# Moving the scaling of s, a piece of statistics, silu stores and a load of gates, and merging two copies of u, in a bidirectional scan layer

## The chip, the cores and the metric

The kernel runs on one core of one Trainium2 chip. The metric is the device time of a whole launch in microseconds (us). The profile is one execution recorded by the hardware profiler. Engines are named as in its views: PE is TensorE's matmul, PEld its weight load, ACT ScalarE, DVE VectorE, POOL GpSimd, SP (or SPq) SyncE, which here issues nearly all transfers.

## The reference

The input x has 4 images of 128 channels and 96 x 96 pixels. It is group-normalised (32 groups), read as four sequences of 9216 positions (rows forward, rows backward, columns forward, columns backward), and each goes through the same layer:

```python
t = grouped1x1(x, in_proj_w, in_proj_b, 4)        # 128 -> 512 channels
u, gate = t[:, :256], t[:, 256:]
u = silu(u)
u = depthwise_conv(u, dw_w, K=5)
s  = ssm_in_w @ u                                  # 256 -> 32, as the next three
a  = clip(0.999 + 0.0009 * sigmoid(ssm_delta_w @ u + b), 0.0001, 0.9999)
bb = tanh(ssm_b_w @ u + b)
cc = tanh(ssm_c_w @ u + b)
prefix = cumsum(log(a))
h = exp(prefix) * cumsum(bb * s * exp(-prefix))    # h[n] = a[n] * h[n-1] + bb[n] * s[n]
u = u + ssm_out_w @ (cc * h + ssm_d * s)
u = grouped1x1(u * sigmoid(gate), mix_w, mix_b, 4)
y = out_proj_w @ u + out_proj_b
```

The four results are put back in pixel order, joined to 512 channels, multiplied by `fuse_w` (128 x 512), and added to x.

## The kernel before, in words

**Tiling.** All data is fp32. The work of an image is two phases, vertical ("V", columns) and then horizontal ("H", rows); so there are 8 phases, numbered 0 to 7. Each phase runs two streams side by side: s = 0 reads the sequence forward, s = 1 the same sequence backward. A phase has 6 steps (`NS`), and a step has four pairs (`R`). A pair is a tile of 384 positions (every fourth position of 1536) of both streams. So there are 24 pairs in a phase and 192 in all, numbered t = 0 to 191; k is t mod 4.

**Second halves are not computed anew.** The backward stream meets in the second half of a phase what the forward stream met in the first, and the other way round. So in_proj with its silu (`compute_front`, L476) and the gates (`gate`, L487, `sigmoids`, L509) run only for steps 0 to 2 of a phase ("fresh"). Gates of the first ten pairs of a phase are stored to DRAM (L518) and loaded back for their mirrored pairs (`load_kept`, L526); the last two pairs' gates stay in two buffers, `gates[0]` and `gates[1]`, which the loads use too. The silu of steps 0 and 1 is stored (`keep_silu`, L452, 770 KB for a quarter of a step) and loaded back (`load_silu`, L458). The silu tile `sil` has two buffers, so step 2 is written where step 0 was.

**One pair.** `pair(t)` works on pair t at its front end and on pair t - 6 (`LAG`) at its back end. "old" means that the back end's pair is in the second half of its phase, "with_front" that in_proj for pair t + 4 runs here, and "ahead" that the pair is old or has no in_proj. By position in a phase, pairs 20 to 23 and 0 to 5 are old with in_proj, 6 and 7 have in_proj and gates, 8 to 17 have gates and no in_proj, and 18 and 19 are old without in_proj. The parts of a pair, with their names and lines, are:

- `front`: in_proj of pair t + 4 into banks 7, 6, 2, 3, its silu on ACT (L476), loads of the next step's x_in (L252), and stores of silu.
- `taps` (L611, DVE, and L609, ACT): the convolution's second half of the channels, five taps. The first tap is written to PSUM by ACT a pair ahead (`first_tap`).
- `conv` and `conv_less`: the first half of the channels as matmuls with banded matrices ("band", then "less"), L133 being the helper that records every matmul of 32 columns. L594 copies the results of both streams to SBUF as u.
- `proj` (L133, "main"): the four small projections into banks 4 and 5, read by ACT as tm (L639), a copy of s (L640) and a tanh (L641). POOL makes a of it (L644) and bb * s (L647), and `scale_s` (L664, ACT) then multiplies s by ssm_d in place.
- `scan` (L681, DVE), two calls a step, and `outputs` (L687 to L689, POOL), five pairs later.
- `out_of` (L493): ssm_out_w into banks 0 to 3, onto u that ACT has copied there (`under`, L501).
- `gating` (L563, DVE), reading gates and banks 0 to 3. Banks 0 and 1 are also those of the first tap, so ACT's first tap waits for it.
- `accumulate` (L133, "w_fin"): mix, out_proj and fuse_w in one product, copied by ACT as ys (L712, L714) and added to acc by POOL (L728).

**What sets the order.** The order of instructions on each engine is written out by hand: the pairs run under a manual schedule, so each engine and SyncE's queue carry out instructions in the order in which the program names them. Only semaphores between engines are added.

**Banks.** With in_proj, `conv` uses banks 4 and 5 (`PROJ`); without it banks 7 and 6 (`FRONT[:2]`), stream 0 in bank 7 and stream 1 in bank 6. The gates of such a pair go to banks 4, 5, 7, 6 (`GATE[False]`), so the third and fourth gate matmul wait until u has been copied out of 7 and 6.

**Statistics.** The next image's normalisation is prepared on the side: in V phases chunks of x are loaded (L393) and reduced (L397, DVE) in pairs with k > 1, and `stats_finish` is a generator whose pieces are called in the H phase, one in each pair with k > 1 (`stats_piece`); some of the pieces have matmuls (L186, L198, L234).

The lines that decide where the changed parts stand are these:

```python
if ahead:
    accumulate(waiting.pop(0), w[1])()
    free[0] = w[0]
    stats_piece()

    other = nc.vector.tensor_copy if k > 1 and not old else nc.scalar.copy
    conv_less(i, banks, (nc.scalar.copy, other))
...
    first_tap(i + 2)
    scale_s(i - 2)
```

Of the kernel before, what the change touches and what calls it, by code (L numbers as in the profile page):

```python
# [55 lines left out]
R = 4  # L56
LN = 16
NS = HH // LN
N = LN * WW // R
# [7 lines left out]
def conv_preact_kernel(  # L67
# [60 lines left out]
    def bank(i):  # L128
        return psum[:, i, :]

    def mm(o, col, lhsT, rhs, start, stop):
        r = slice(32 * col, 32 * col + 32)
        nc.tensor.matmul(o[r, : rhs.shape[-1]], lhsT, rhs, start=start, stop=stop,  # L133
                         skip_group_check=True)
# [183 lines left out]
    def less_of(p):  # L318
        return 1 if p < 2 else 0
# [93 lines left out]
    def front(i, banks):  # L413
        for _ in front_parts(i, banks):
            pass

    def front_parts(i, banks):

        step, g = divmod(i, R)
        if step * UB >= NU:  # L420
            return
        st = step % NS
        if st == NS // 2:
            sils[step] = sils[step - 1]
            load_silu(step + 1, (g,))
        elif st == NS - 1 and g < 2:
            load_silu(step, (2 * g, 2 * g + 1))
        elif g == 0 and fresh(step):
            sils[step] = wk.tile([P, 2, 2, 4, N + 1], F32, tag="sil", name=f"sil_{step}")
        if fresh(step):  # L430
            yield from compute_front(step, g, banks)
        sil = sils[step]

        if st == 0:
            engine = nc.gpsimd if step else nc.vector
            for s in range(2):
                engine.memset(sil[64 * s : 64 * s + 64, s, 0, g, 0:1], 0.0)
            if g < 2:
                engine.memset(sil[:, :, 1, g, 0:1], 0.0)

        for s in range(2):
            load_front(step + 1, s, slice(64 * s + 32, 64 * s + 64), slice(g, g + 1))
        if g == R - 1:
            for s in range(2):
                load_front(step + 1, s, slice(64 * s, 64 * s + 32), slice(0, R))
        if step:
            keep_silu(step, g)

    def keep_silu(step, g):
        st = step % NS  # L450
        if st < NS // 2 - 1:
            nc.sync.dma_start(kept_sil[step // NS % 2][st][g], sils[step][:, :, :, g, :])  # L452

    def load_silu(step, gs):
        if 0 in gs:
# [111 lines left out]
    def columns(step, sil, k):  # L567

        if fresh(step):
            return sil[..., k : k + N]  # L570
        return sil[..., 1 - k : 1 - k + N][..., ::-1]

    def blocks(step):
        return [sils[step][:, s if fresh(step) else 1 - s, 0] for s in range(2)]

    def conv(i, banks):

        step, p = units[i]["step"], units[i]["p"]
        sil, k = blocks(step), less_of(p)
        for s in range(2):  # L580
            for g in range(4):
                mm(bank(banks[s]), g, band[:, s, p, g, :], columns(step, sil[s][:, g, :], 1 - k),
                   True, False)

    def conv_less(i, banks, copies=(nc.scalar.copy, nc.scalar.copy)):
        step, p = units[i]["step"], units[i]["p"]
        sil, k = blocks(step), less_of(p)
        for g in range(4):
            for s in range(2):
                r = less_rows(s, p)  # L590
                mm(bank(banks[s]), g, less[r, p, g, :], columns(step, sil[s][r, g, :], k),
                   False, True)
        for s, copy in enumerate(copies):
            copy(us[i][:, s, 0, :], bank(banks[s])[:, :N])  # L594

    def new_u(i):
        us[i] = wk.tile([P, 2, 2, N], F32, tag="u", bufs=LAG + 2, name=f"u_{units[i]['id']}")
# [64 lines left out]
    def scale_s(i):  # L662
        s = tbs[i][0:64, :]
        nc.scalar.activation(s, s, AF.Copy, scale=d_sb[0:64, 0:1])  # L664
# [68 lines left out]
        return add  # L733


    later = []

    waiting = []

# [7 lines left out]
    def pair(t):  # L747
# [9 lines left out]
        banks, w = plan(with_front or not back)  # L757
        if back:
            front(t + R, FRONT)
        if seed and not with_front:  # L760
            under(bi, 1)
        send()
# [19 lines left out]
        def stats_piece():  # L782
            if later and k > 1:
                next(later[0], None)
# [11 lines left out]
        if ahead:  # L796
            accumulate(waiting.pop(0), w[1])()
            free[0] = w[0]
            stats_piece()

            other = nc.vector.tensor_copy if k > 1 and not old else nc.scalar.copy
            conv_less(i, banks, (nc.scalar.copy, other))
        if old:
            for s in range(2):
                for j in range(2):
                    out_of(bi, s, j)
                load_gate(bi + s + UB)
        elif back:
            gates_and_out(bi, with_front)
# [168 lines left out]
```

## Time and profile before

| | |
|---|---|
| time, median of 3 runs | 1869.76 us (1868.79 to 1873.79) |
| span of the profiled execution | 1866.4 us, mean granted TensorE clock 0.990 |
| busy: PE, DVE, ACT, POOL | 98%, 84%, 83%, 84% |
| bytes read and written in DRAM | 185 MB and 132 MB, 170 GB/s over the span |
| silu stores and loads (L452, L458) | 128 of 770 KB, 6.2 us to landing |
| stores of gates (L518) | 80 of 768 KB, 3.9 us |
| loads of kept gates (L526) | 76 of 768 KB, 5.0 us |
| copies of u (L594) | 352 on ACT, 482 ns; 32 on DVE, 550 ns |
| copy of 128x768 on ACT (L501) | 352, 802 ns |
| scaling of s (L664) | 192, 601 ns |

A row of the profile's groups names line, engine, operation, the tile written and those read, shapes and count; then the busy time, the mean of one, and the idle time of its engine just ahead of it with what ended it. A row of the timeline is a start, a duration, the engine, the line and the tiles, "xN" for several in a row, and in brackets the idle time before. A matmul of fp32 shows as two records. Durations of matmuls include the time in which the next one already runs, so what a group costs is read from start to start.

### The profile page before, as it was taken

The numbers are of one execution on the slowest core, as the hardware profiler recorded it, in microseconds if no ns is written. First come the engines' busy times: TensorE is split into PE (matmuls) and PEld (weight loads), VectorE is DVE, ScalarE is ACT, GpSimd is POOL, SyncE is SP. The second block draws the span as 40 slices with busy tenths as digits, with TensorE's granted clock in tenths as the row PEclk, the third lists the DMA queues.
The fourth block names the chain that finished last, engine by engine and source line by source line (L and its number), as shares of the span: only waits on it lengthen the run. The fifth ranks groups of instructions, "written<-read, shape, count | busy, mean of one in ns | idle before, by whom it ended". The sixth has DMA issues, their size and how long they took to land.

```text
span 1866.4 us, 57669 instructions
## 1 busy us (share of the span) xinstructions
PE 1827.3 (98%) x24024; PEld 691.4 (37%) x24024; DVE 1561.9 (84%) x1573; ACT 1542.6 (83%) x2841; POOL 1567.0 (84%) x1615
## 2 busy tenths in 40 slices
PE   6899999999999999999999999999999999999998
PEld 3234333443334433344333433334333443334432
DVE  4698878888888988888889898888887888878886
ACT  4688888888888888888888888888888888888875
POOL 6388988888879899888887989888888889997886
PEclk7999999999999999999999999999999999999999
DMA  5564463433875557243596556433467634535424
GB/s 194 162 197 145 146 207 118 168 141 126 274 244 202 169 155 215 86 158 131 186 301 217 167 162 207 152 130 126 139 224 234 231 113 156 191 118 175 145 102 171
DMA packets 147828, 321.21 MB, mean 172 GB/s; under 512 B 14192, under 2 KB 115696, under 8 KB 147568
## 3 DMA queue, kind: packets, MB, share of 16 engines
q1 hardware_dynamic: 147136, 316.56, 51.5%
q8 instruction: 190, 3.11, 0.7%
q10 hardware_dynamic: 432, 0.96, 0.1%
q14 instruction: 70, 0.57, 0.1%
HBM read 185.21 MB, written 132.25 MB: 170 GB/s over the span
## 4 chain that ended last, share of the span: by engine, by line
PE 87%; ACT 4%; POOL 3%; DVE 2%; DMA 1%; issue 1%; SPq 0%; POOLq 0%; DVEq 0%; ACTq 0%
PE psum L133 73%; PE psum L487 7%; PE psum L493 7%; ACT sil L476 1%; DMA xs<-in_xr 1%; ACT psum L609 1%; DVE u L563 1%; DVE psum L611 1%; POOL acc L728 1%; POOL t L644 1%; ACT u L594 0%; POOL t L647 0%; DMA x_in<-in_xs 0%; POOL t L687 0%; POOL t L688 0%
## 5 line engine op out<-in xcount | busy, mean ns | idle before, releaser
L611 DVE SCALAR_TENSOR_TENSOR psum<-sil,small,psum 128x768 f32<-128x768 f32 x576 | 589.0, 1023 | 39.1 <-ACT psum L609 13.5
L133 PE MATMUL psum<-u,w_fin 128*32 128x384 f32 x6144 | 535.6, 488 | 0.0
L133 PE MATMUL psum<-u,main 128*32 128x384 f32 x6144 | 534.9, 489 | 0.3 <-DVE u L611 0.3
L563 DVE SCALAR_TENSOR_TENSOR u<-gate,psum 128x768 f32<-128x768 f32 x376 | 349.9, 952 | 165.9 <-ACT u L594 91.6
L728 POOL TENSOR_TENSOR acc<-ys,acc 128x384 f32<-128x384 f32 x376 | 412.7, 1118 | 21.6 <-ACT ys L714 4.3
L687 POOL TENSOR_TENSOR t<-t,t 64x384 f32<-64x384 f32 x192 | 263.8, 1374 | 78.0 <-DVE t L681 58.0
L133 PEld LDWEIGHTS psum<-u,w_fin 128*32 128x32 f32 x6144 | 195.9, 110 | 303.3 <-issue 223.6
L501 ACT COPY psum<-u 128x768 f32<-128x768 f32 x352 | 277.6, 802 | 34.9 <-DVE u L611 28.8
L133 PE MATMUL psum<-sil,band 128*32 128x384 f32 x3072 | 291.9, 494 | 10.8 <-ACT tm L639 8.2
L133 PEld LDWEIGHTS psum<-u,main 128*32 128x32 f32 x6144 | 181.8, 109 | 324.9 <-issue 203.0
L644 POOL TENSOR_SCALAR t<-tm 64x384 f32<-64x384 f32 x191 | 177.9, 931 | 133.0 <-ACT tm L639 103.2
L688 POOL TENSOR_TENSOR t<-t,t 64x384 f32<-64x384 f32 x192 | 276.3, 1439 | 15.1
L609 ACT ACTIVATE psum<-sil,small 128x768 f32<-128x768 f32 x192 | 174.1, 907 | 104.6 <-DVE u L563 98.6
L493 PE MATMUL psum<-t,main 32*128 32x384 f32 x1536 | 240.2, 520 | 3.3 <-POOL t L688 1.5
L647 POOL TENSOR_TENSOR t<-t,tm 64x384 f32<-64x384 f32 x192 | 208.9, 1088 | 15.3
L509 ACT ACTIVATE gate<-psum,bnorm 128x384 f32<-128x384 f32 x384 | 194.8, 583 | 13.9 <-PE psum L487 7.7
L476 ACT ACTIVATE sil<-psum,bnorm 128x385 f32<-128x385 f32 x384 | 192.0, 585 | 11.7 <-DMA xs<-in_xr 5.4
L611 DVE SCALAR_TENSOR_TENSOR u<-sil,small,psum 128x768 f32<-128x768 f32 x192 | 194.9, 1015 | 7.8
L487 PE MATMUL psum<-x_in,wn 32*128 32x384 f32 x768 | 193.8, 521 | 0.5 <-ACT u L594 0.3
L594 ACT COPY u<-psum 128x384 f32<-128x384 f32 x352 | 153.1, 482 | 30.1 <-PE psum L133 21.8
L714 ACT COPY ys<-psum 128x384 f32<-128x384 f32 x287 | 132.5, 475 | 49.5 <-PE psum L133 41.5
L133 PE MATMUL psum<-sil,less 64*32 64x384 f32 x3072 | 168.8, 497 | 0.0
(87 smaller groups left out, 1642.0 us busy)
## 6 DMA issues: line engine op xcount, KB each, us to landing
sil<-sil SPq DMA_DIRECT2D x128, 770.0 KB, 6.2
kept<-gate SPq DMA_DIRECT2D x80, 768.0 KB, 3.9
gate<-kept SPq DMA_DIRECT2D x76, 768.0 KB, 5.0
x_in<-in_xs SPq DMA_DIRECT2D x192, 96.2 KB, 2.5
out<-acc SPq DMA_DIRECT2D x48, 384.0 KB, 6.1
acc<-in_xr SPq DMA_DIRECT2D x38, 384.0 KB, 6.3
xs<-in_xr SPq DMA_DIRECT2D x72, 192.0 KB, 5.1
x_in<-in_xs SPq DMA_DIRECT2D x184, 48.1 KB, 4.7
```

The source lines that it names most:

```text
L133: nc.tensor.matmul(o[r, : rhs.shape[-1]], lhsT, rhs, start=start, stop=stop, skip_group_check=True)
L476: nc.scalar.activation(sil[:, s, j, g, :], bank(banks[2 * s + j])[:, : N + 1], AF.Silu, bias=bn[:, 1:2] if j else bn[:, 4 + g : 5 + g],)
L487: nc.tensor.matmul(bank(to)[:, :N], stats[un["b"]][0][r, s, :], x_in[s][r, q, off : off + N], start=True, stop=True)
L493: nc.tensor.matmul(bank(SSM + 2 * s + j)[:, :N], w_so[r, bass.ts(j, P)], z[r, :], start=bi not in seeded, stop=True, skip_group_check=True)
L501: nc.scalar.copy(psum[:, SSM + 2 * s : SSM + 2 * s + 2, :N], us[bi][:, s])
L563: nc.vector.scalar_tensor_tensor(v, g, 1.0, pz, ALU.add, ALU.mult)
L611: nc.vector.scalar_tensor_tensor(us[i][:, :, 1, :] if k == K - 1 else part, src, w_tap[:, k : k + 1], part, ALU.mult, ALU.add,)
L644: nc.gpsimd.tensor_scalar(*op)
L647: nc.gpsimd.tensor_mul(ta[0:64, p, :], tb[0:64, :], tm[0:64, :])
L687: nc.gpsimd.tensor_mul(ta[0:64, p, :], tb[64:P, :], ta[64:P, p, :])
L688: nc.gpsimd.tensor_add(tb[0:64, :], ta[0:64, p, :], tb[0:64, :])
L728: adder.tensor_add(part, y, part)
```

## The change

The change has six edits. They leave every matmul and every byte moved as they are.

- **Stores of silu** go through a list, `to_keep`. Step 0's four stores are issued at the end of pairs 0, 1 (two) and 2, in place of one at the end of each of pairs 0 to 3. Step 1's wait until step 2's in_proj (pairs 4 to 7), one each. In later phases a store is issued at once, as before. This is to spread the transfers of the first pairs.
- **Banks of conv**: stream s is put in the lower bank plus s, so without in_proj stream 0 is in bank 6 and stream 1 in 7.
- **One copy of u**: without in_proj both banks are copied by one ACT instruction, 128 x 2 x 384, in place of two (the second on DVE in pairs with k > 1 that aren't old). With in_proj there are two copies on ACT as before.
- **Statistics' piece**: in old pairs it is called after `conv_less` and no longer ahead of it.
- **Load of kept gates**: from pairs with k = 2 it is put off to the next pair, behind that pair's in_proj and its loads of x_in (`soon`).
- **Scaling of s**: in old pairs it stands ahead of `out_of`, before the first tap; in all others behind `proj`. Before, pairs with a back end had it between the first tap and `proj`.

```diff
         if g == R - 1:
             for s in range(2):
                 load_front(step + 1, s, slice(64 * s, 64 * s + 32), slice(0, R))
-        if step:
-            keep_silu(step, g)
-
-    def keep_silu(step, g):
-        st = step % NS
         if st < NS // 2 - 1:
-            nc.sync.dma_start(kept_sil[step // NS % 2][st][g], sils[step][:, :, :, g, :])
+            to_keep.append((step, g))
+        if step > 1:
+            keep_silu(1)
+
+    to_keep = []
+
+    def keep_silu(n):
+        for step, g in to_keep[:n]:
+            nc.sync.dma_start(kept_sil[step // NS % 2][step % NS][g], sils[step][:, :, :, g, :])
+        del to_keep[:n]
...
     def conv(i, banks):
 
         step, p = units[i]["step"], units[i]["p"]
-        sil, k = blocks(step), less_of(p)
+        sil, k, b0 = blocks(step), less_of(p), min(banks)
         for s in range(2):
             for g in range(4):
-                mm(bank(banks[s]), g, band[:, s, p, g, :], columns(step, sil[s][:, g, :], 1 - k),
+                mm(bank(b0 + s), g, band[:, s, p, g, :], columns(step, sil[s][:, g, :], 1 - k),
                    True, False)
 
-    def conv_less(i, banks, copies=(nc.scalar.copy, nc.scalar.copy)):
+    def conv_less(i, banks):
...
-        for s, copy in enumerate(copies):
-            copy(us[i][:, s, 0, :], bank(banks[s])[:, :N])
+        if banks == PROJ:
+            for s in range(2):
+                nc.scalar.copy(us[i][:, s, 0, :], bank(b0 + s)[:, :N])
+        else:
+            nc.scalar.copy(us[i][:, :, 0, :], psum[:, b0 : b0 + 2, :N])
...
-    later = []
+    later, soon = [], []
...
         if back:
             front(t + R, FRONT)
+        for n in soon:
+            load_kept(n)
+        soon.clear()
...
         if ahead:
             accumulate(waiting.pop(0), w[1])()
             free[0] = w[0]
+            if not old:
+                stats_piece()
+            conv_less(i, banks)
+        if old:
             stats_piece()
-
-            other = nc.vector.tensor_copy if k > 1 and not old else nc.scalar.copy
-            conv_less(i, banks, (nc.scalar.copy, other))
-        if old:
+            scale_s(i - 2)
             for s in range(2):
                 for j in range(2):
                     out_of(bi, s, j)
...
         if back:
-            load_kept(bi // 2 + 2)
+
+            if k == 2 and t + 1 < NU // 2:
+                soon.append(bi // 2 + 2)
+            else:
+                load_kept(bi // 2 + 2)
...
             first_tap(i + 2)
-            scale_s(i - 2)
...
         proj(i, PROJ)
-        if not back and t > 0:
+        if not old and t > 0:
             scale_s(i - 2)
...
-        if t < R:
-            keep_silu(0, t)
+
+        keep_silu((1, 2, 1, 0)[t] if t < R else 0)
```

More of the change, by code (lines that the diff above doesn't have):

```diff
@@ L578, in conv @@
         step, p = units[i]["step"], units[i]["p"]
-        sil, k = blocks(step), less_of(p)
+        sil, k, b0 = blocks(step), less_of(p), min(banks)
         for s in range(2):
             for g in range(4):
-                mm(bank(banks[s]), g, band[:, s, p, g, :], columns(step, sil[s][:, g, :], 1 - k),
+                mm(bank(b0 + s), g, band[:, s, p, g, :], columns(step, sil[s][:, g, :], 1 - k),
                    True, False)
-    def conv_less(i, banks, copies=(nc.scalar.copy, nc.scalar.copy)):
+    def conv_less(i, banks):
         step, p = units[i]["step"], units[i]["p"]
-        sil, k = blocks(step), less_of(p)
+        sil, k, b0 = blocks(step), less_of(p), min(banks)
         for g in range(4):
@@ L590, in conv_less @@
                 r = less_rows(s, p)
-                mm(bank(banks[s]), g, less[r, p, g, :], columns(step, sil[s][r, g, :], k),
+                mm(bank(b0 + s), g, less[r, p, g, :], columns(step, sil[s][r, g, :], k),
                    False, True)
-        for s, copy in enumerate(copies):
-            copy(us[i][:, s, 0, :], bank(banks[s])[:, :N])
+        if banks == PROJ:
[3 more added lines that the diff above has]
+            nc.scalar.copy(us[i][:, :, 0, :], psum[:, b0 : b0 + 2, :N])
     def new_u(i):
```

## The prediction

> **What bounds the kernel now.** I read the page first (busy shares, chain), then the timeline of a steady pair, and then looked for pairs longer than that.
>
> ```profile
> PE 1827.3 (98%) x24024; PEld 691.4 (37%) x24024; DVE 1561.9 (84%) x1573; ACT 1542.6 (83%) x2841; POOL 1567.0 (84%) x1615
> ...
> PE 87%; ACT 4%; POOL 3%; DVE 2%; DMA 1%; issue 1%; SPq 0%; POOLq 0%; DVEq 0%; ACTq 0%
> ```
>
> TensorE is busy for 98% of the span and is 87% of the chain that ended last; every other engine has a sixth of its time free. The timeline of a steady pair in the second half of a phase (an old pair) with in_proj shows what a pair costs when nothing waits:
>
> ```profile
> 489.88 2.79 PE L133 MATMUL psum<-u,main 128*32 128x384 f32 x32
> ...
> 492.60 0.94 PE L133 MATMUL psum<-x_in,wn 32*32 32x385 f32 x32
> ...
> 493.47 1.50 PE L133 MATMUL psum<-sil,band 128*32 128x384 f32 x16
> ...
> 494.79 2.77 PE L133 MATMUL psum<-u,w_fin 128*32 128x384 f32 x32
> ...
> 497.48 0.88 PE L133 MATMUL psum<-sil,less 64*32 64x384 f32 x16
> ...
> 498.29 0.93 PE L493 MATMUL psum<-t,main 32*128 32x384 f32 x8
> ...
> 499.15 1.18 PE L133 MATMUL psum<-u,main 128*32 128x384 f32 x12
> ```
>
> From proj to proj: 499.15 - 489.88 = 9.27 us, and each group starts where the one before it ends. So a pair's floor is its matmuls: start to start, proj 2.72, in_proj 0.87, band 1.32, w_fin 2.69, less 0.81, state 0.86. I then took the start of every first tap (L609, one a pair, 192 of them) and differenced them. Most differences are 9.25 to 9.33; pairs that hold both in_proj and gates have 10.15, the two light pairs of a phase 8.3. Phases 1 to 6 (of 0 to 7, 24 pairs each) last 229.8, 224.5, 226.7, 224.6, 226.9 and 223.4 us; the last of these is nearly free of stalls. Against it the others have lost 6.4, 1.1, 3.3, 1.2 and 3.5, together 15.5 us, and the first phase has a loss of its own. A change that adds no TensorE work can win back those places and little else. They are these.
>
> The start:
>
> ```profile
> 63.81 1.25 SPq L452 DMA_DIRECT2D sil<-sil  x2
> ...
> 69.30 2.79 PE L133 MATMUL psum<-u,main 128*32 128x384 f32 x32
> ...
> 74.75 2.00 ACT L476 ACTIVATE sil<-psum,bnorm 128x385 f32<-128x385 f32 x4 [5.36 <-DMA xs<-in_xr]
> ...
> 77.27 2.79 PE L133 MATMUL psum<-sil,band 128*32 128x384 f32 x16 [5.18 <-ACT tm L639]
> ...
> 79.99 1.53 PE L133 MATMUL psum<-sil,less 64*32 64x384 f32 x16
> ```
>
> ScalarE waits 5.36 us before the first silu of step 2, which is written into the buffer that held step 0. The page puts this down to a chunk of x, but a silu doesn't read it; what it must wait for is the last store of step 0's silu, one of the two issued from 63.81, behind six other stores of 770 KB. TensorE idles 5.18 us and then runs slowly: band takes 79.99 - 77.27 = 2.72 where it took 1.32.
>
> The first phase boundary:
>
> ```profile
> 244.61 0.47 SPq L526 DMA_DIRECT2D gate<-kept  x1
> ...
> 245.19 2.40 SPq L252 DMA_DIRECT2D x_in<-in_xs  x4
> ...
> 255.52 0.88 PE L133 MATMUL psum<-x_in,wn 32*32 32x385 f32 x16 [0.87 <-DMA x_in<-in_xs]
> ...
> 256.33 2.79 PE L133 MATMUL psum<-sil,band 128*32 128x384 f32 x16
> ```
>
> A load of kept gates (768 KB) is queued just ahead of the four loads of x_in, whose rows TensorE then waits for (0.25 and 0.87 us), and again the band after it takes 258.87 - 256.33 = 2.54.
>
> The vertical phases with chunks of x:
>
> ```profile
> 622.18 0.54 DVE L594 COPY u<-psum 128x384 f32<-128x384 f32 x1
> ...
> 622.78 0.29 PEld L487 LDWEIGHTS psum<-x_in,wn 32*128 32x128 f32 x2 [0.69 <-DVE u L594]
> ```
>
> The copy of u that VectorE makes stands behind two statistics (L397, 621.25 to 622.27), and the last gate matmul waits 0.69 us for its bank.
>
> [...] the granted clock is 0.50 from 76 to 82 us and from 257 to 259 us, after both waits, though the second was only 1.1 us of reported idle; so a removed wait also gives back the slow matmuls after it. [...]
>
> **The change part by part.**
>
> Stores of silu. Step 1's four stores leave the stretch before 66 us and go to pairs 4 to 7; step 0's four are issued by the end of pair 2 instead of pair 3. By bytes, 4 x 0.77 = 3.1 MB of the 6.2 MB of stores leave a stretch in which the DMA view shows all engines nine tenths busy at some 280 GB/s; 3.1 MB are 11 us of it. The last store of step 0 would be issued near 57 to 59 and land some 6 us later (median 6.2), before 68 when the silu could start. So the wait goes: 5.18 on TensorE. With it go the slow matmuls: band 2.72 - 1.32 = 1.40, less 1.46 - 0.81 = 0.65, in_proj 1.26 - 0.87 = 0.39, together 2.44. Sum 7.6. In the same pair in_proj waited 1.20 for x_in and VectorE 1.68 for a chunk of x; they overlap with one another and end in about 0.8 on the path, of which I count nothing, since the order of the rest is tight. Take 7.5; bounds 5 (the wait alone) and 9. The postponed stores meet little: DMA is idle from 76 to 90 us.
>
> Load of kept gates after the next in_proj (three of ten loads per phase). At the first boundary x_in no longer stands behind 768 KB. The transfers landing between 248.5 and 255.4 us show the gates first (252.7), then x_in (252.9 to 255.4); 768 KB at 200 to 300 GB/s are 2.6 to 3.8 us, so x_in would land by about 252 and in_proj could start at 253.5. Saved: waits 1.12, band 2.54 - 1.32 = 1.22, w_fin 3.16 - 2.69 = 0.47, together 2.8 (bounds 1.1 and 3.7, that pair's whole excess of 12.96 over 9.26). The other boundaries (10.37, 10.61, 10.03) show no wait for x_in: nothing there. The gates are needed a pair later; 5 us to landing is hidden by 9.27 us of matmuls. On SyncE the load now stands behind x_in, no longer x_in behind a load that waits for VectorE's gating.
>
> One copy of u. In the 12 pairs of a phase without in_proj, 2 x 482 ns become one copy of 128x768; L501 moves the same shape in 802 ns. Where VectorE made the second (32 times) it loses 550 ns and ScalarE gains 802 - 482 = 320. Against: the third gate matmul waits for 802 ns and not 482. But the sigmoids start only when the first gates are done (858.71 while the copy ended at 858.41), the fourth gate waited for the second copy anyway, and proj waits for the first sigmoid's bank; pairs where ScalarE already made both copies in a row (0.86 us) take the same 9.30. So I take nothing for it (bounds 0 and 0.3 us in 80 pairs). For: the pairs where VectorE's copy was late. In the last six pairs without in_proj of the three vertical phases with chunks, the excess over 9.30 is 0.5, 0.75 and 0.8: 2.0. The pairs that hold pieces of the statistics in the horizontal phases show the same wait once each, about 0.2: 0.5 more. Sum 2.5.
>
> Scaling of s (L664, 601 ns). In old pairs it moves ahead of the first tap, where ScalarE idles 1.02 us for VectorE's gating: hidden, and it leaves the stretch between the tap and tm. It needs the product of the pair before (L647), which ended before ScalarE would get there in all but four old pairs, where it is 0.3 to 0.5 us late; 0.16 at most comes of it. In pairs that aren't old it goes behind proj's three evictions; tm, its copy and POOL's decay come 0.6 us earlier. In a steady pair TensorE is the limit and nothing is won. Where a late gating has made the tap late (the boundary pairs 24, 72, 120, 168 and the statistics pairs 27, 75, 123) band waits for tm: some 0.3 of 0.6 in seven places, 2.0.
>
> Statistics' matmuls behind less, in old pairs only, so at one piece per batch with a matmul: TensorE no longer waits for the copy of ys (0.45 to 1.1 us, three times), but VectorE's chain behind that matmul (mean, dev, ex, gm, 290.76 to 293.46) starts 0.3 later, and the gating behind it sets the next tap. I take 0 (bounds -1 and +2.5).
>
> Sum: 7.5 + 2.8 + 2.5 + 2.0 = 14.8; 1869.8 - 14.8 = 1855.0 us.
>
> **The rivals.** (1) The waits move rather than go: the silu of step 2 waits for whichever of its four stores lands last, and if chunks and x_in keep the engines full, half of the 7.5 stays; the boundary keeps its half-clock window. Then about 5 us, 1865. For it: the wait ended only when all DMA had drained. Against: 3.1 MB fewer in the queue. (2) Slower: the single copy holds the third gate, and with it proj, back by the full 0.29 us (a copy ending at 858.78 in place of 858.41, gate at 858.83 in place of 858.54) in 80 pairs: +23 - 14.8 = +8, 1878. For it: these pairs are at TensorE's limit, with no slack. Against: the pairs with two copies in a row, as said. (3) More: the excess of all boundary and statistics pairs goes too: 15.5 in phases 1 to 5 and 9 at the start, 1845.
>
> **How the numbers follow.** The forecast gets 0.68, rival 1 0.14, rival 2 0.06, rival 3 0.12. The bounds of the start (5 to 9), of the boundary (1.1 to 3.7), of the copy (-3 to +3) and of the rest make 1847 to 1864 for the likeliest and most of 1 and 3. Faster by over 5.6 us: the forecast, rival 3 and half of rival 1: 0.87; within: 0.07; slower: 0.06.
>
> **What would show it.** Right: no wait over 1 us before a silu (L476's successor) near 68 us; granted clock 1.0 from 50 us on, and in the pair after the first boundary; no VectorE copy of u at all; ScalarE's idle time ahead of the first tap in old pairs falls from 1.02 to some 0.4 with the scaling in it; steady pairs stay at 9.27 and 9.30. Wrong: pairs without in_proj at 9.4 or more (rival 2), a wait of the silu or of x_in that is only shorter (rival 1), or a gating that waits for kept gates.

## The result, and the profile after

The changed kernel takes 1852.45 us, the median of 4 runs (1852.26 to 1853.45), against 1870.35 (1868.79 to 1873.79) for the kernel before. The ratio is 0.9903, with a 95% interval of 0.9886 to 0.992. The forecast was 1855.0. The spans of the two profiled executions are 1850.7 and 1866.4 us, 15.7 apart; the granted clock is 0.992 and was 0.990.

From the page of the changed kernel, busy time and shares of the chain, and one row of the DMA issues (the last number is the median time to landing):

```profile
PE 1817.3 (98%) x24024; PEld 695.5 (38%) x24024; DVE 1549.8 (84%) x1541; ACT 1587.2 (86%) x2773; POOL 1561.3 (84%) x1615
...
PE 92%; ACT 3%; POOL 2%; DVE 1%; issue 0%; POOLq 0%; DVEq 0%; ACTq 0%
...
gate<-kept SPq DMA_DIRECT2D x76, 768.0 KB, 6.7
```

TensorE's share of the chain rose from 87% to 92%, and DMA is no longer named in it. VectorE has 32 instructions fewer (its copies of u), ScalarE 68 fewer. The kept gates now land 6.7 us after issue, it was 5.0; nothing in the chain waits for them.

Where the time went is read from the starts of the first taps (L616 now). I call the difference from one first tap to the next the row of a pair, and add up the 24 rows of each phase (the last phase has 23). The line "before, again" is a second profile of the kernel before, from another run.

```
phase           0      1      2      3      4      5      6      7
before        219.2  229.8  224.5  226.7  224.6  226.9  223.4  211.7
before, again 221.8  230.2  224.5  227.0  226.4  226.8  223.7  211.7
after         210.4  224.8  224.9  224.8  224.9  224.8  224.9  211.3
after - before -8.8   -5.0   +0.4   -1.9   +0.3   -2.1   +1.5   -0.4
```

The first two phases bring 13.8, the horizontal ones after them 4.4. The vertical phases 2, 4 and 6 have become longer, which the prediction did not foresee. A row moves by some 0.02 us from one profile to the next where nothing waits. But phase 0 of the kernel before differs by 2.6 between its two profiles, in the rows of pairs 0 and 3, and phase 4 by 1.8, where one pair had a stall of its own. Two places are uneven in many profiles: the row of pair 0 is anywhere from 7.3 to 8.3, and pairs 98 and 99 together take 18.5 in most profiles and up to 18.98 in others.

The start, in the timeline of the changed kernel (start, duration, engine, line, tiles, idle time before in brackets):

```profile
55.78 0.53 SPq L455 DMA_DIRECT2D sil<-sil  x1
...
64.16 1.25 SPq L455 DMA_DIRECT2D sil<-sil  x2
...
67.56 2.79 PE L133 MATMUL psum<-u,main 128*32 128x384 f32 x32
...
68.20 1.03 SPq L455 DMA_DIRECT2D sil<-sil  x1
68.31 2.00 ACT L480 ACTIVATE sil<-psum,bnorm 128x385 f32<-128x385 f32 x4
...
70.83 1.78 PE L133 MATMUL psum<-sil,band 128*32 128x384 f32 x16 [0.48 <-ACT tm L646]
...
72.54 0.88 PE L133 MATMUL psum<-sil,less 64*32 64x384 f32 x16
```

The last store of step 0 is issued at 55.78 and lands at 63.97. The first two stores of step 1 follow at 64.16, the third at 68.20. The silu of step 2 starts at 68.31 with no wait, where it waited 5.36; band waits 0.48 in place of 5.18, and less takes 0.88 in place of 1.53. The same stretch in the windows (stretch, its length, busy time of PE, PEld, DVE, ACT and POOL, granted clock, DMA share, GB/s):

```profile
66.00:70.00 4.00, 4.00 (x80) 1.30 (x64) 2.81 (x3) 3.28 (x7) 1.02 (x1) 1.00 1.12 244
70.00:74.00 4.00, 3.44 (x72) 0.81 (x64) 3.90 (x4) 2.79 (x7) 2.86 (x3) 1.00 1.04 275
74.00:78.00 4.00, 4.00 (x85) 1.30 (x69) 3.90 (x4) 3.97 (x9) 2.34 (x2) 1.00 0.51 155
```

The clock stays at 1.00. The DMA engines still move 155 GB/s from 74 to 78 us, where they moved 11 in the kernel before: the transfers are spread and not gone.

The first boundary, in the same timeline:

```profile
236.19 2.18 SPq L252 DMA_DIRECT2D x_in<-in_xs  x4
...
241.18 2.95 SPq L530 DMA_DIRECT2D gate<-kept  x2
...
244.45 1.01 PE L133 MATMUL psum<-x_in,wn 32*32 32x385 f32 x32
...
245.39 1.50 PE L133 MATMUL psum<-sil,band 128*32 128x384 f32 x16
```

The loads of x_in now stand ahead of the kept gates; in_proj begins without a wait and band is at its usual 1.50.

A pair of a vertical phase with statistics:

```profile
608.12 1.02 DVE L397 BATCH_NORM_STATS2 bn<-xs 128x6 f32<-128x384 f32 x2
...
608.35 0.80 ACT L601 COPY u<-psum 128x768 f32<-128x768 f32 x1
```

The one copy of u runs on ScalarE beside the statistics of VectorE, where VectorE's copy stood behind them.

And the new wait, at pair 56, the first of those in phase 2 that have gates and no in_proj:

```profile
545.23 1.47 PE L133 MATMUL psum<-u,w_fin 128*32 128x384 f32 x16
...
545.98 0.58 ACT L648 ACTIVATE t<-psum,small 64x384 f32<-64x384 f32 x1
...
546.58 0.61 ACT L671 ACTIVATE t<-t,small 64x384 f32<-64x384 f32 x1
547.22 0.48 ACT L721 COPY ys<-psum 128x384 f32<-128x384 f32 x1
...
547.75 1.50 PE L133 MATMUL psum<-sil,band 128*32 128x384 f32 x16 [1.05 <-ACT ys L721]
```

In the kernel before the same instructions stood so:

```profile
558.25 0.60 ACT L664 ACTIVATE t<-t,small 64x384 f32<-64x384 f32 x1
...
558.76 1.47 PE L133 MATMUL psum<-u,w_fin 128*32 128x384 f32 x16
...
559.70 0.58 ACT L641 ACTIVATE t<-psum,small 64x384 f32<-64x384 f32 x1
...
560.05 1.64 PE L133 MATMUL psum<-sil,band 128*32 128x384 f32 x16
...
560.30 0.48 ACT L714 COPY ys<-psum 128x384 f32<-128x384 f32 x1
```

At a change of image (pairs 55, 103 and 151) one w_fin stands behind proj, and its bank must be emptied through ys. Now the scaling (L671) stands directly ahead of that copy (before, L664 stood ahead of tm), and band's stream 0 goes into bank 6, the very bank that this w_fin has filled. Band, which had begun 0.25 before the copy of ys, now begins 0.53 after it.

### The profile page after: what moved, and what is told of

It reads as the page before. It is cut to its first block, busy times and chain, and to the rows that moved or that the text cites. A ratio compares the mean times of both kernels' runs of the same rounds, so it can differ in the third digit from the quotient of the medians.

```text
span 1850.7 us, 57595 instructions
## 1 busy us (share of the span) xinstructions
PE 1817.3 (98%) x24024; PEld 695.5 (38%) x24024; DVE 1549.8 (84%) x1541; ACT 1587.2 (86%) x2773; POOL 1561.3 (84%) x1615
## 4 chain that ended last, share of the span: by engine, by line
PE 92%; ACT 3%; POOL 2%; DVE 1%; issue 0%; POOLq 0%; DVEq 0%; ACTq 0%
PE psum L133 78%; PE psum L497 7%; PE psum L491 7%; ACT sil L480 1%; ACT psum L616 0%; ACT u L599 0%; POOL acc L735 0%; POOL t L651 0%; POOL t L694 0%; ACT t L648 0%; ACT tm L646 0%; POOL t L695 0%; POOL t L654 0%; ACT t L671 0%; DVE u L567 0%
## 5 line engine op out<-in xcount | busy, mean ns | idle before, releaser
L616 ACT ACTIVATE psum<-sil,small 128x768 f32<-128x768 f32 x192 | 174.2, 907 | 55.4 <-DVE u L567 54.5
L513 ACT ACTIVATE gate<-psum,bnorm 128x384 f32<-128x384 f32 x384 | 199.7, 579 | 4.0 <-PE psum L497 1.6
L491 PE MATMUL psum<-x_in,wn 32*128 32x384 f32 x768 | 189.0, 531 | 1.3 <-ACT u L599 1.3
L133 PEld LDWEIGHTS psum<-sil,band 128*32 128x32 f32 x3072 | 89.2, 109 | 184.0 <-issue 75.4
```

The lines of the kernel that those rows point to most:

```text
L491: nc.tensor.matmul(bank(to)[:, :N], stats[un["b"]][0][r, s, :], x_in[s][r, q, off : off + N], start=True, stop=True)
L513: nc.scalar.activation(gv[:, s, j, :], bank(banks[2 * s + j])[:, :N], AF.Tanh, bias=bn[:, 2 + j : 3 + j], scale=0.5,)
```

## The experiments

Times are medians with their range. The kernel before ran beside every group of runs, with a median between 1868.87 and 1872.92 that differs by group; so parts worth less than 3 us are told apart by the rows of pairs, and ratios stand beside them. Runs e1 to e7, e6b and e11 are the changed kernel with the edit shown; e8 and e9 are the kernel before with one part of the change, and e10 is the kernel before itself.

**Stores of silu as before (e1).**

```diff
-        if st < NS // 2 - 1:
+        if step and st < NS // 2 - 1:
             to_keep.append((step, g))
-        if step > 1:
             keep_silu(1)
...
-        keep_silu((1, 2, 1, 0)[t] if t < R else 0)
+        if t < R:
+            to_keep.append((0, t))
+            keep_silu(1)
```

> The changed kernel with the silu stores as before (step 0's at the end of pairs 0 to 3, step 1's at once). Theory: the early stores' queue makes the first silu of step 2 wait, and the half clock follows from that; the time rises by 8 us (the sum of the rows of pairs 3, 4 and 5) to about 1860.5, with a wait of about 5 us ahead of that silu and a granted clock of 0.5 for one or two windows. Rival: the first phase gained because u, taps and scaling run otherwise; then the time stays within 2 us of 1852.5 and no such wait appears.

1861.73 us (1861.2 to 1862.26), ratio to before 0.996 (0.9945 to 0.9974), span 1859.5, so 8.8 above the changed kernel's profile. Phase 0 is back at 219.6, all other phases stay where the change put them (224.7 to 224.9 and 211.2). Pairs 3 to 6 take 40.9 us; before they took 40.05, after the change 31.77. The stores account for the whole of phase 0. Pair 24, though, stays at 10.16: it does not need the stores' part.

**The load of kept gates at once (e2).**

```diff
-            if k == 2 and t + 1 < NU // 2:
-                soon.append(bi // 2 + 2)
-            else:
-                load_kept(bi // 2 + 2)
+            load_kept(bi // 2 + 2)
```

> The changed kernel with every load of kept gates issued at once. Theory: x_in of the first boundary (pair 24) again stands behind 768 KB, in_proj waits about 1 us for it and the clock drops for a window; pair 24 takes 12.5 to 13 us in place of 10.26, the time rises by 2 to 3 us to about 1855. Rival: the wait in pair 24 was a matter of when the first phase's transfers ran, 9 us later than now, and is gone whatever the order of the two loads; then the time stays at 1852.5 within 0.5.

1854.12 us (1852.38 to 1856.97), ratio 0.992 (0.9906 to 0.9935), span 1851.1, 0.4 above. Pair 24 has 10.19, against 10.26 with the load put off and 12.96 before. The 0.4 of span doesn't come from there: the row of pair 52 is 10.16 in this profile, where it was 9.33, and the same rows of phases 4 and 6 keep their 9.33. So beside the other edits the rows show nothing for this one.

**Two copies of u, the second on VectorE where it was (e3).**

```diff
-            nc.scalar.copy(us[i][:, :, 0, :], psum[:, b0 : b0 + 2, :N])
+            for s, copy in enumerate((nc.scalar.copy, other)):
+                copy(us[i][:, s, 0, :], bank(b0 + s)[:, :N])
...
-            conv_less(i, banks)
+            conv_less(i, banks, nc.vector.tensor_copy if k > 1 and not old else nc.scalar.copy)
```

> The changed kernel with two copies of u in pairs without in_proj, the second on VectorE where k > 1 and the pair isn't old, the banks as changed. Theory: VectorE's late copies come back in pairs 11 to 16 of the phases with chunks and in the pairs with pieces of statistics; the time rises by 2 to 3 us to about 1855, and pairs without them stay at 9.27. Rival: the one copy holds back the third gate in 80 pairs; then two copies make the steady pairs without in_proj shorter by 0.05 to 0.3 us each and the time falls to 1830 to 1849.

1857.06 us (1856.28 to 1857.67), ratio 0.9936 (0.9919 to 0.9952), span 1854.6, 3.9 above. Pairs 9 to 17 of each phase add up to this:

```
phase      0      1      2      3      4      5      6
one copy 83.46  84.14  83.40  84.14  83.39  84.14  83.40
two      84.02  84.87  84.03  84.80  84.13  84.80  83.24
before   84.23  84.77  84.49  84.83  84.55  84.78  83.20
```

The groups of both kernels, busy time and mean ns of one, then idle time before. The changed kernel:

```profile
L601 ACT COPY u<-psum 128x768 f32<-128x768 f32 x100 | 79.9, 799 | 7.0 <-PE psum L133 3.1
```

This run:

```profile
L602 ACT COPY u<-psum 128x384 f32<-128x384 f32 x168 | 73.8, 482 | 7.3 <-PE psum L133 3.1
L602 DVE COPY u<-psum 128x384 f32<-128x384 f32 x32 | 17.6, 549 | 5.8 <-PE psum L133 5.7
```

One copy of 768 columns costs 799 ns, two of 384 cost 964. Phase 6 is the control: it has no statistics, and there two copies are 0.16 shorter. The rows with both copies on ScalarE are 9.31 or 9.32 against 9.26 or 9.27, but a second copy on a free VectorE wins more than that back (rows of 9.05). So the net gain, 0.56 to 0.74 a phase, is there only where VectorE has statistics to do.

**Scaling of s as before (e4).**

```diff
         if old:
             stats_piece()
-            scale_s(i - 2)
...
             first_tap(i + 2)
+            scale_s(i - 2)
...
-        if not old and t > 0:
+        if not back and t > 0:
             scale_s(i - 2)
```

> The changed kernel with the scaling of s between first tap and proj wherever a pair has a back end, as before. Theory: the pairs at the start of horizontal phases lose 1.1 us each phase again (rows 0 to 4: 47.1 to 48.2), four times, and pairs 56, 104 and 152 (12.04) get 0.6 shorter, since the late copy of ys no longer stands behind the scaling; the time rises by 2 to 3 us to about 1855. Rival: the place of the scaling only matters for ScalarE's load and changes nothing at TensorE's limit; within 0.5 us of 1852.5.

1854.1 us (1853.41 to 1855.64), ratio 0.992 (0.9905 to 0.9935), span 1851.7, 1.0 above. The sum hides two signs. Phases 1, 3, 5 and 7 are 0.6, 0.7, 0.6 and 1.0 longer than in the changed kernel, together 2.95. In phases 2, 4 and 6 the two rows around the new wait (pairs 55 and 56, 103 and 104, 151 and 152) are 0.94 to 0.96 shorter, together 2.85. So by the rows the scaling's gain and loss nearly cancel. The 1.0 of span lies in pair 0 and in pairs 98 and 99 (some 0.46 each), the two uneven places; nothing ties it to the edit. The rows of pairs 56, 104 and 152 are 11.29, 11.27 and 11.59, against 12.04 after the change and 10.64, 10.63 and 10.95 before. So the scaling is part of the new wait of band, and not all of it: 0.63 to 0.65 remain with the scaling where it was.

**The statistics' piece ahead of less (e5).**

```diff
-            if not old:
-                stats_piece()
+            stats_piece()
             conv_less(i, banks)
         if old:
-            stats_piece()
```

> The changed kernel with the statistics' piece ahead of less in old pairs too, as before. Theory as in the prediction: VectorE's chain behind that matmul starts 0.3 earlier, TensorE waits 0.5 for ys instead; rows 3 and 4 of the three horizontal phases with statistics keep their sum of 18.9 within 0.3, the time is within 1 us of 1852.5. Rival: the wait of TensorE counts, the sum becomes 19.5 and the time 1854 to 1855.

1853.52 us (1852.91 to 1853.84), ratio 0.9896 (0.988 to 0.9912), span 1852.0. This ratio cannot tell it from the changed kernel. The rows can: the two rows of pairs 3 and 4 of phases 1, 3 and 5 add up to 19.28, against 18.90 after the change, and the row of pair 6 gives 0.14 back (10.32, 10.46). That is 0.23 a phase and 0.7 in all. The rest of the 1.3 of span lies in phases without such a piece, so it isn't the edit's.

**Both halves of the new wait removed (e6).** The scaling stands behind the late ys, and stream 1's band goes first, as its bank 7 is free:

```diff
-        for s in range(2):
+        for s in (0, 1) if banks == PROJ else (1, 0):
             for g in range(4):
...
         proj(i, PROJ)
-        if not old and t > 0:
-            scale_s(i - 2)
         if late:
             add()
             accumulate(waiting.pop(0), w[1])()
+        if not old and t > 0:
+            scale_s(i - 2)
```

> The changed kernel with two instructions moved: in the pair that changes image (t = 55, 103, 151) the scaling of s behind the late copy of ys, and in pairs without in_proj the band of stream 1 (bank 7) ahead of that of stream 0 (bank 6). Theory: in pairs 56, 104 and 152 band no longer waits 1.05 us for bank 6, the rows fall from 12.04 to about 10.7 and the time by 3 to 4.5 to about 1848.5. Rival: those pairs are long because ScalarE and VectorE are late there (first tap, add, gating), and TensorE waits elsewhere instead; rows stay above 11.7 and the time within 1 us of 1852.5.

1850.22 us (1849.42 to 1850.92), ratio 0.9903 (0.9888 to 0.9917). Its span of 1847.7 is the shortest of all profiles, 3.0 below the changed kernel's. Its timeline at pair 56:

```profile
545.51 1.47 PE L133 MATMUL psum<-u,w_fin 128*32 128x384 f32 x16
...
546.80 1.69 PE L133 MATMUL psum<-sil,band 128*32 128x384 f32 x16
...
547.10 0.48 ACT L721 COPY ys<-psum 128x384 f32<-128x384 f32 x1 [0.27 <-PE psum L133]
547.61 0.61 ACT L671 ACTIVATE t<-t,small 64x384 f32<-64x384 f32 x1
```

Band starts 1.29 after w_fin, with no wait. The rows of pairs 56, 104 and 152 are 11.01, 11.00 and 11.00, and phases 2, 4 and 6 are 223.9 each, 1.0 below the changed kernel; 3 x 1.0 is the 3.0 of the span. In time the two kernels were measured in different groups, and their intervals overlap: the gain is shown in the rows, not by the ratio.

**The order of the streams alone (e6b).** Only the first hunk of the edit above.

> The changed kernel with only the band of stream 1 (bank 7) ahead of stream 0 in pairs without in_proj; the scaling stays ahead of the late copy of ys. Theory: 0.66 us of band then covers all but 0.4 of the wait in pairs 56, 104 and 152; rows of 11.4 to 11.6, the time about 1851. If the bank order alone makes the wait: rows of 11.0 as with both moves, 1850. If the scaling alone: 12.0, 1852.5.

1851.48 us (1851.41 to 1852.33), ratio 0.9887 (0.987 to 0.9903), span 1849.8. The three rows are 11.39, 12.11 and 11.39. Two of three win 0.65 of the 1.04 that both hunks together win: band's wait falls from 1.05 to 0.40 in all three pairs. In the middle one the gain is lost again. VectorE's and POOL's rows at pair 56 of this run, and at pair 104:

```profile
548.78 2.40 POOL L735 TENSOR_TENSOR acc<-ys,acc 128x384 f32<-128x384 f32 x2
...
549.96 2.83 DVE L688 TENSOR_TENSOR_SCAN t<-t,t 64x768 f32<-64x768 f32 x1
...
998.29 3.92 POOL L735 TENSOR_TENSOR acc<-ys,acc 128x384 f32<-128x384 f32 x2
...
999.40 1.82 DVE L688 TENSOR_TENSOR_SCAN t<-t,t 64x768 f32<-64x768 f32 x1
```

At pair 56 the scan starts 1.18 after the start of POOL's two additions, at pair 104 only 1.11 after it. There the scan is a us shorter and the additions 1.5 longer, and the next copy of ys then waits 1.28 for a buffer that they still hold.

**Step 0's last store a pair later (e7).** The postponement of step 1's stores stays; step 0's go out one a pair.

```diff
-        keep_silu((1, 2, 1, 0)[t] if t < R else 0)
+        keep_silu(1 if t < R else 0)
```

> The changed kernel with step 0's silu stores at the end of pairs 0, 1, 2 and 3, one each, and step 1's still put off. Theory that the length of the queue made the wait: with 3.1 MB fewer ahead of it the last store, issued near 64, lands near 69, and the silu waits at most 1 us: about 1853. Theory that the place of step 0's last store made it: the store cannot be issued before the in_proj of pair 3 and x_in's four loads (0.96 MB with it), it lands 6 to 7 us later, the silu waits 2 to 3 us: about 1855.5.

1855.6 us (1853.88 to 1855.88), ratio 0.9929 (0.9912 to 0.9945), span 1854.2, 3.5 above. Its timeline:

```profile
64.60 2.68 SPq L455 DMA_DIRECT2D sil<-sil  x3
...
68.27 2.79 PE L133 MATMUL psum<-u,main 128*32 128x384 f32 x32
...
70.83 2.00 ACT L480 ACTIVATE sil<-psum,bnorm 128x385 f32<-128x385 f32 x4 [1.67 <-PE psum L133]
...
73.35 2.45 PE L133 MATMUL psum<-sil,band 128*32 128x384 f32 x16 [2.29 <-ACT tm L646]
```

The bracket puts the silu's wait down to a matmul, but in_proj had long been done. The last store of step 0, issued in the group at 64.60, landed at 70.75, and the silu started at 70.83. In the kernel before that store landed at 74.57 and the silu started at 74.75. Twice the start follows the landing by 0.08 to 0.18, so this is the wait, although neither bracket names it. Both parts of the edit count: with step 1's stores out of the queue the landing comes 3.8 sooner (proj of that pair only 1.0 sooner), and with step 0's earlier issue the wait is gone.

**Two parts of the change alone on the kernel before**: the load put off (e8, shown here), and the stores (e9, whose edit is the first and the last hunk of the change).

```diff
+        for n in soon:
+            load_kept(n)
+        soon.clear()
...
-            load_kept(bi // 2 + 2)
+            if k == 2 and t + 1 < NU // 2:
+                soon.append(bi // 2 + 2)
+            else:
+                load_kept(bi // 2 + 2)
```

> The kernel before with the put-off load of kept gates alone. Theory as in the prediction: x_in of pair 24 lands before 768 KB of gates, its wait and the half clock behind it go, pair 24 falls from 12.96 to about 10.2, the time by 2.8 to about 1866.5. Rival, after the run with the loads at once: pair 24 is near the edge and a shift in the first phase's transfers decides it; then the order of loads alone may leave 12 us or more there, and the time stays within 1 us of before.

1867.18 us (1866.5 to 1870.79), ratio 0.9994 (0.9985 to 1.0002), which includes no difference; span 1864.9. In its profile pair 24 has 10.57, though.

> The kernel before with the stores of silu changed alone. Theory: the first phase falls from 219.2 to about 211, the time by 8 to 9; if the shift of the first phase also frees pair 24, by 11 to 12, to about 1858; if only the order of the loads frees it, pair 24 keeps 12.96 and the time is about 1861.

1858.85 us (1857.66 to 1862.84), ratio 0.9953 (0.9938 to 0.9968). Phase 0 is 211.8, and pair 24 has 10.55. (Its profiled execution had a stall of some 4 us in phase 4, so its span of 1861.1 isn't used.)

The kernel before again, profiled a second time (e10):

> The kernel before, unchanged, for a second profile of it. Theory: the wait for x_in in pair 24 (12.96 in the first profile) belongs to the kernel before and comes again, 12.5 or more, and each of two edits alone would free it. Rival: it was an episode of that one execution; pair 24 takes about 10.5, as in the runs with one edit alone, and the 2.4 us of it are no part of the gain.

Pair 24 has 13.29 here and had 12.96, and pair 27 has 10.90 and had 10.94, against 10.02 in e8 and e9. So the stall was there in both profiles, and pair 27 is long together with pair 24. In_proj of pair 24, in this profile:

```profile
257.47 1.77 PE L133 MATMUL psum<-x_in,wn 32*32 32x385 f32 x32 [1.47 <-DMA x_in<-in_xs]
...
259.17 2.79 PE L133 MATMUL psum<-sil,band 128*32 128x384 f32 x16
```

With the load put off (e8):

```profile
254.78 1.01 PE L133 MATMUL psum<-x_in,wn 32*32 32x385 f32 x32
```

With the stores alone (e9):

```profile
246.32 1.47 PE L133 MATMUL psum<-x_in,wn 32*32 32x385 f32 x32 [0.34 <-DMA x_in<-in_xs]
```

Either part alone frees the pair, in its own way. These are single profiles, but e1 and e2, each without one of the two parts, agree (10.16 and 10.19). From the first issue of the four x_in loads to the last landing it takes 10.2 and 10.3 us in the two profiles of the kernel before, 9.1 with the stores alone, 7.7 with everything but the load's move, and 5.9 and 6.0 where the load is put off. The load's move changes the order in the queue, and order counts: in the profile of the kernel before all 876 of SyncE's transfers landed in the order of their issue, and in that of the changed kernel too. With the stores alone the rows still come behind the gates, about a us sooner; the wait of 0.34 is followed by no fall of the clock (1.00 from 244 to 251 us), and band is not slowed. The landings give the wait: in_proj's first half starts when the third of the four loads is in (landed at 257.42 in the second profile of the kernel before, start at 257.47; 246.28 and 246.32 with the stores alone). That landing comes 9.5 and 8.6 us after the first issue, and in_proj was due at 8.1 and 8.3. Why the loads land sooner with the stores alone was not settled.

**The scaling where each kind of pair had it best (e11).** Stream 1 first; scaling as changed in old pairs, and as before in other pairs with a back end.

```diff
-        for s in range(2):
+        for s in (0, 1) if banks == PROJ else (1, 0):
...
             first_tap(i + 2)
+            if not old:
+                scale_s(i - 2)
...
-        if not old and t > 0:
+        if not back and t > 0:
             scale_s(i - 2)
```

> The changed kernel with bank 7's band first, and the scaling of s ahead of out_of in old pairs (as changed) but between first tap and proj in the other pairs with a back end (as before). Theory: keeps the gain at the start of horizontal phases, and takes row 7 from 10.34 and 10.21 back to 10.15 and row 8 of the vertical phases to 11.0 or less, as the scaling in pairs 54, 55 no longer delays silu and ys; about 1848.5 to 1850. Rival: the late tm of those pairs costs as much; then 1851 to 1852.

1851.83 us (1848.37 to 1853.97), ratio 0.9886 (0.9867 to 0.9904), span 1850.1. The rows of pairs 56, 104 and 152 are 12.12, 12.13 and 10.94: two of three are no better than after the change. Yet band waits for nothing in any of them. At pair 56:

```profile
546.05 1.63 PE L133 MATMUL psum<-sil,band 128*32 128x384 f32 x16
...
548.49 3.83 POOL L735 TENSOR_TENSOR acc<-ys,acc 128x384 f32<-128x384 f32 x2
...
549.49 1.84 DVE L688 TENSOR_TENSOR_SCAN t<-t,t 64x768 f32<-64x768 f32 x1
...
552.36 0.48 ACT L721 COPY ys<-psum 128x384 f32<-128x384 f32 x1 [1.41 <-POOL acc L735]
```

It is again the pair of long additions and short scan, 3.83 and 3.81 at pairs 56 and 104, and 2.40 at pair 152, the one that is fast and has no such wait of the last ys. So a row of 12 us at this place has two causes that look alike in the sum: band's wait for ys, which the change brought and e6 takes away, and the way POOL's second addition meets the scan. The rows of pairs 55, 103 and 151 came down to 10.16 and 9.84 as expected, but the four horizontal phases are 0.2 to 0.4 longer than after the change, most of it in their first row (10.57 to 10.64, against 10.24 to 10.26). That loss was not traced.

## Why the prediction was right, and where it was not

The forecast of 14.8 us stands against 15.7 between the spans and 17.9 between the medians. Undone one at a time, the parts cost 8.8 (stores), 0.4 (load), 3.9 (copy), 1.0 (scaling) and 1.3 (statistics) of span, 15.4 in all. That this is near 15.7 is chance. In the rows the load has nothing, the scaling about 0.1 and the statistics' piece 0.7; the rest of their spans are single stalls. And the stall of pair 24, at least 2.4 us with 0.9 more in pair 27, shows in no undo, since the stores' edit and the load's each remove it. So the total of the forecast came out better than its terms, and in part by luck.

**Stores of silu, 7.5.** Right in mechanism and nearly in size: 8.3 in the rows of pairs 3 to 6, 8.8 in the undo. The wait and the slow matmuls after it went together, as the sum had them (the granted clock is 1.00 from 66 to 78 us, and was 0.50 from 75.48 to 82.31); the 0.8 that I left out for the waits of x_in and of a chunk is the size of what is missing, though no run separates it. Rival 1 asked whether the waits would only move. The silu's wait did come back when one store was issued a pair later (e7), so it was the stores' landing and neither x nor the matmul that the brackets name. One reading was off: step 1's stores did not all leave the stretch before 66 us. Two are issued from 64.16, but now behind step 0's last store, and that order is what counts.

**Load of kept gates, 2.8.** Pair 24 did get shorter by what was foretold, 12.96 to 10.26, which is 2.7. But the term was credited to this edit alone, and the sum treated the terms as independent. The stores' edit alone gives the same pair 10.55, and on top of the others the load's move shows nothing in this row (10.19 without it in e2). Rival 1, a boundary that keeps its slow clock, is not what happened with the stores alone (granted clock 1.00 from 244 to 251 us) or with the load's move alone (1.00 from 254 to 261). What failed is the independence of the two terms.

**One copy of u, 2.5.** It brought 3.9. The term for the vertical phases with chunks, 2.0, was right: 0.56, 0.63 and 0.74 are 1.9. The term for the horizontal phases was mis-sized: I took 0.5 for the one wait a phase that I had seen, and e3 shows 0.73, 0.66 and 0.66, together 2.05. The statistics' pieces delay VectorE's copy in more pairs than the one read. Rival 2, that the merged copy would hold the third gate by 0.29 in 80 pairs, is refuted: the pairs that had been at 9.30 now have 9.26 or 9.27. On ScalarE one copy takes 964 - 799 = 165 ns less than two. I had weighed the single copy against the first of two (482) and not against both; where ScalarE had made both, the pair gained 0.04 and lost nothing.

**Scaling of s, 2.0.** It brought about 0.1 by the rows of e4, because the working had only its gains. These were there: 0.6 to 0.7 in each of phases 1, 3 and 5, and 1.0 in phase 7. ScalarE's idle time ahead of the first tap fell, as said, if less far. The waits view (us in all, times, longest) of the kernel before:

```profile
ACT psum L609 <- DVE u L563: 98.6, 92, 2.3
```

Of the changed kernel:

```profile
ACT psum L616 <- DVE u L567: 54.5, 90, 1.4
```

That is 1.07 down to 0.61 a time. The failed step is "In pairs that aren't old it goes behind proj's three evictions ... In a steady pair TensorE is the limit and nothing is won". I did not ask what is queued behind the scaling there. In three pairs it is the copy of ys at the change of image. I had also passed over the swap of the two banks as if it cost nothing: it puts band's first stream into the bank that this copy must empty. The two together made a wait of 1.05 where there was none, and some 0.95 in each of phases 2, 4 and 6 are the scaling's share by e4. The swap's share shows in e6b, 0.65 where it helped, and in e4, 0.63 to 0.65; the two overlap and can't be added.

**Statistics' piece, 0.** By the rows of e5 it brought 0.7, inside the bounds of -1 and +2.5. The wait saved weighed more than the later chain on VectorE.

**What would show it.** No VectorE copy of u is left, no wait over 1 us before a silu at 68 us, and the granted clock is 1.00 there (66 to 78 us) and at pair 24 (236 to 262). Steady pairs are at 9.27, those without in_proj too, where 9.30 was foretold. No gating waits for kept gates, though they land 1.7 later.

## What to carry to other kernels

When TensorE is the limit, difference the starts of one instruction that each unit of work has once: the longer units name the stalls, and undoing an edit shows in those rows at a tenth of a microsecond where run times differ by three. Before moving an instruction or swapping two buffers, look through the rare units too (first, last, change of image), and ask what is queued behind the new place and who still holds the new buffer. Where two edits relieve the same wait, either may take all of it, as at pair 24 (12.96, and 10.57 or 10.55 with one edit): count that wait once, and give the second edit nothing.

## What the hardware showed that was not expected

The granted clock fell after waits of little more than 1 us. In the profile of the kernel before it is 0.50 from 75.48 to 82.31 us, a fall that begins within band's wait of 5.18, and again from 256.39 to 259.80, at pair 24, after only 0.25 and 0.87 us of reported wait. In the second profile the wait at pair 24 is 1.47, and the mean clock from 254 to 261 us is 0.87. With the stores alone and a wait of 0.34 the clock stays at 1.00, and so it does around band's wait of 1.05 at pairs 56, 104 and 152 of the changed kernel (1.00 from 546 to 553, 996 to 1003 and 1446 to 1453 us). The windows, with columns as above (the granted clock is the third number from the end), of the kernel before:

```profile
254.00:261.00 7.00, 6.13 (x72) 1.91 (x60) 5.52 (x4) 4.49 (x9) 6.60 (x7) 0.76 0.78 252
```

Of its second profile:

```profile
254.00:261.00 7.00, 5.51 (x72) 1.51 (x66) 5.37 (x7) 5.43 (x10) 6.53 (x8) 0.87 0.91 255
```

And of the kernel with the stores alone, whose pair 24 comes earlier:

```profile
244.00:251.00 7.00, 6.66 (x104) 2.27 (x95) 5.29 (x6) 6.54 (x12) 6.61 (x7) 1.00 0.88 274
```

In the first of these the fall at pair 24 lasts 3.41 us. By estimate, 3.41 x 0.50, it costs up to 1.7 us of TensorE's work beside the wait itself, more than the wait (1.12 by the two reports). These two falls of that profile begin and end at whole multiples of 3.413 us from one another (75.48, 82.31, 256.39 and 259.80). Which waits bring a fall on, and whether their place against these marks counts beside their length, these runs don't show.

The other surprise is the meeting of POOL's additions and VectorE's scan in e6b and e11. It has two outcomes. In one, the two additions take 2.40 and the scan 2.83, and POOL's next product 2.54. In the other the additions take 3.92, the scan 1.82 and the next product 1.19 (pairs 56 and 104 of e6b). Which of POOL's instructions is the slow one differs, and the last copy of ys behind them waits (1.28 to 1.41) in the second case alone. The slow one ends 1.00 us after the scan at pair 56 (553.79 and 552.79, the product) and 0.99 after it at pair 104 (1002.21 and 1001.22, the second addition). Which of them starts first doesn't decide it: POOL's second addition starts 0.07 after the scan at pair 104 of e6b, where it is long, and 0.08 after it at pair 152 of e11, where it isn't. That POOL's instruction is held until the scan ends is an estimate from these ends; no run takes the scan away.
